# Two gathers for the left-over edges: accumulate in the DMA, or land in two halves and add on VectorE

## The chip, the cores and the metric

The kernel runs on one core of a Trainium2 chip. The metric is the device time of one execution in microseconds (us). Of the kernel before, three timed runs are given, 3217.1, 3209.39 and 3217.16 us, with a median of 3217.1 us. A fourth execution was profiled: it took 3212.38 us, with a span of 3210.7 us between its first and its last instruction and a mean granted TensorE clock of 0.993.

Five engines work side by side and meet at semaphores: TensorE (PE in the profile, PEld its weight loads), VectorE (DVE), ScalarE (ACT), GpSimd (POOL) and SyncE (SP). In this kernel SP issues the plain DMAs and POOL issues the indirect ones, the gathers.

## What is computed

The input is 64 graphs of 256 nodes with 256 features each, and one adjacency matrix for all of them, with few edges. Four layers run one after the other; layers 0, 1 and 3 are of one kind, layer 2 is an attention. Of the first kind, what matters here is the edge score S:

```python
pre_u = jnp.einsum('bud,dk->buk', h_t, W1[:d])
pre_v = jnp.einsum('bvd,dk->bvk', h_t, W1[d:])
hidden = jax.nn.relu(pre_u[:, :, None, :] + pre_v[:, None, :, :] + b1)
S = jax.nn.sigmoid(jnp.einsum('buvk,ko->buvo', hidden, W2)[..., 0] + b2[0])
a_t = jnp.einsum('buv,bud->bvd', S * A_a, h_t)
m_t = jnp.einsum('uv,bud->bvd', A_m, h_t) * h_t
z_t = beta1 * h_t + beta2 * (jnp.einsum('bvd,de->bve', a_t, Wa) + ba) + beta3 * (jnp.einsum('bvd,de->bve', m_t, Wm) + bm)
```

S is multiplied by A, so only the scores of edges that exist are needed. For each edge (u, v) that is a row of pre_u plus a row of pre_v, a relu, and a dot product with W2.

## The kernel before

Two graphs are worked on together, as a pair. Two streams of 16 pairs, "a" and "b", run interleaved. For each pair and each of the three layers with edge scores, `before` makes both projections and writes them to two tables in HBM (`tableu` and `tablev`, 256 rows each, one row for each node with both graphs side by side; SP, L750, one DMA for each table and each block of 128 rows). `scores` then makes the edge scores and `after` uses them. There are 16 x 2 x 3 = 96 such scorings. While one stream is in `scores`, which is heavy on VectorE, the other does its `after`, its attention and its next `before`, which are heavy on TensorE. The order of both on PE, DVE and ACT is written out by hand, one string for each kind of stage (`PLAN`): each letter runs one step of one generator, and `tc.manual_schedule` keeps that order on these three engines. R is the step `rest`, the one this study is about.

After the start the same six scorings come again every 195 us or so, 16 times. The texts below call them places 1 to 6, in order of time:

- place 1: the third layer of "b", under plan (LAST, "a"); place 2: the first layer of the next pair of "a", under (LAST, "b");
- place 3: the first layer of "b", under (GNN[0], "a"); place 4: the second layer of "a", under (GNN[0], "b");
- place 5: the second layer of "b", under (GNN[1], "a"); place 6: the third layer of "a", under (GNN[1], "b"). In places 5 and 6 the light stream does its attention.

The edges are cut into 16 blocks of 128. Ten blocks are made on TensorE, by one-hot matrices (`made`, into the PSUM tile `ga`). Six blocks (`FETCHED`) are gathered from the tables by indirect DMA into the SBUF tile `fetched`. Edges for which a block had no room, at most 64 for a graph, are the left-over edges: 128 rows for two graphs, of 256 elements, in the SBUF tile `left`. Each gathered block takes two gathers: one writes the rows of one table over the tile (`compute_op` bypass), the second adds the rows of the other table to it while it lands (`compute_op` add). `left` is made in the same way: `left<-tableu` writes, `left<-tablev` adds.

All gathers are issued by POOL in one order, that of `fetches_of`: `fetch` ties each one behind the one before it (`tc.issue_after`). Call the six blocks a to f. For each scoring the order is: u(a), u(b), v(c), v(d), then v(a) and v(b) that add, as soon as block 0 of the tables is written; then, once block 1 is written, `left<-tableu`, u(c) and u(d) that add, `left<-tablev` that adds, u(e), u(f), and v(e) and v(f) that add. An adding gather waits for the landing of the gather that wrote its tile. The two adding gathers of c and d stand between the two of `left`.

On VectorE the sum of each edge is worked off by one instruction for each 256 elements (`rated`: relu, times W2, and a running sum into a column of `raw`; the profile's group `junk<-...`). `rest` is one such instruction, on `left`. `rated_all` (steps E and Z) then makes the scores of `raw` on ScalarE (`val`), and `spread` brings them to the matrix `sa` by matmuls `ps<-rm,gu` and `ps<-ro,guo`.

The tile `left` has one buffer for each stream, as `puv` and the parts of it have. All those steps have line 104 in the profile (the helper that records the engine's last instruction), so groups are told apart by their tiles. The gathers have line 858.

Of the kernel before, what the change touches and what calls it, by code (L numbers as in the profile page):

```python
# [8 lines left out]
FP = mybir.dt.float32  # L9
# [3 lines left out]
ALU = mybir.AluOpType  # L13
AX = mybir.AxisListType

P = 128
B, N, D = 64, 256, 256
# [7 lines left out]
REST, DIAGONAL, BLOCKS = 0, 1, 5  # L25
# [21 lines left out]
def fetches_of(l):  # L47

    def part(b, x):
        y = 1 - x if places(b)[0] > places(b)[1] else x  # L50
        return b, x, y

    first, then = [], [(None, 0, 0)]
    for b in FETCHED[l]:
        one = [part(b, x) for x in range(2)]
        (first if min(places(b)) == 0 else then).append(one[0])
        (first if max(places(b)) == 0 else then).append(one[1])
    by = lambda p: p[1]
    first.sort(key=by)
    waiting = [p for p in then if p[0] and p[1] and min(places(p[0])) == 0]  # L60
    last = sorted((p for p in then if p[0] and p not in waiting), key=by)
    return [first, then[:1] + waiting + [(None, 1, 1)] + last]


PLAN = {
# [61 lines left out]
def adj_seq_kernel(ctx: ExitStack, tc: tile.TileContext, a: dict, out: bass.AP):  # L127
# [421 lines left out]
    def few(stack):  # L549
# [173 lines left out]
        def before(st, l):  # L723

            hT = st["hT"]
            st["puv"] = puv = one.tile([P, 2, 2, 2, D], FP, tag="puv", name="puv")
            st["parts"] = parts = [one.tile([P, 2, 2, 2 * D], FR, tag=f"part{k}" + st["side"], name=f"part{k}") for k in range(2)]
            order = [(m, g) for m in range(2) for g in range(2)]
            if l == LAST:
                order = [(m, g) for g in range(2) for m in range(2)]  # L730

            st["tables"] = [
                tables.tile([N, 2 * D], FP, tag="table" + t + st["side"], name="table" + t) for t in "uv"
            ]

            st["fetches"] = []
            st["fetched"] = {b: got_.tile([P, 2, D], FP, tag="fetched", name="fetched") for b in FETCHED[l]}
            st["left"] = one.tile([P, D], FP, tag="left" + st["side"], name="left")
            for m, g in order:
                if l == LAST and (m, g) == (1, 0):  # L740
                    st["flip"](1)
                t = psum()
                for c in range(2):
                    mm(out=t, lhsT=hT[:, c, g, blk(m)], rhs=w1[l][:, c], start=c == 0, stop=c == 1)
                scalar.copy(puv[:, m, 0, g, :], t[:, 0, :])
                vector.tensor_tensor(puv[:, m, 1, g, :], t[:, 1, :], b1row[l], ALU.add)
                if g == 1:
                    x = puv[:, m].rearrange("p w g d -> p (w g d)")
                    for w, rows in enumerate(st["tables"]):
                        nc.sync.dma_start(out=rows[blk(m)], in_=x[:, w * 2 * D : w * 2 * D + 2 * D])  # L750
                    st["fetches"] += fetches_of(l)[m]
                    if numbered:
                        fetch(st)
                    elif st not in unfetched:
                        unfetched.append(st)
                    yield
                    flat = [p[:, m].rearrange("p w d -> p (w d)") for p in parts]
                    for k, h in enumerate(halves):
                        scalar.copy(flat[k][h], x[h])
                    yield  # L760
                    for k, h in enumerate(halves):
                        vector.tensor_tensor(flat[k][halves[1 - k]], x[h], flat[k][h], ALU.subtract)
                yield

        def scores(st, l):

            raw = wk.tile([P, LATE.stop], FP, tag="raw", name="raw")
            val = wk.tile([P, LATE.stop], FP, tag="val", name="val")
            rm = one.tile([P, 2, 8, 2, 64], FP, tag="rm", name="rm")
            ro = one.tile([P, 2, N], FR, tag="ro", name="ro")  # L770
            st["val"], st["rm"], st["ro"] = val, rm, ro
            puv, parts = st["puv"], st["parts"]

            def rated(t, i):
                junk = wk.tile([P, D], FP, tag="junk", name="junk")
                vector.scalar_tensor_tensor(
                    junk, t, 0.0, w2row[l], ALU.max, ALU.mult, accum_out=raw[:, i : i + 1]
                )

            def both(t, *cols):  # L780
                for g in range(2):
                    rated(t[:, g, :], cols[g])

            def tile_scores(t, k, m, i):
                col = BLOCKS + 16 * m + 4 * k + i
                both(t, col, col + 8)

            def rated_all(cols, m):
                scalar.activation(val[:, cols], raw[:, cols], AF.Tanh, bias=halfb2[l], scale=0.5)
                scalar.add(val[:, cols], val[:, cols], 1.0)  # L790
                if m == 0:
                    wt = wk.tile([P, 3], FP, tag="wt", name="wt")
                    wh = wk.tile([P, 1], FR, tag="wh", name="wh")
                    vector.tensor_tensor(wt[:, 0:1], val[:, REST : REST + 1], awo, ALU.mult)
                    vector.tensor_copy(wh, wt[:, 0:1])
                    vector.tensor_tensor(wt[:, 1:2], wt[:, 0:1], wh, ALU.subtract)
                    for g, h in enumerate(halves):
                        for part, o in enumerate((h, halves[1 - g])):
                            scalar.mul(ro[o, g], gvo[h], wt[h, part : part + 1])
                of = slice(BLOCKS + 16 * m, BLOCKS + 16 * m + 16)  # L800
                vector.tensor_tensor(
                    rm[:, m], gva[:, m].rearrange("p k i v -> p (k i) v").unsqueeze(2).to_broadcast([P, 8, 2, 64]),
                    val[:, of].rearrange("p (g x) -> p x g", g=2).unsqueeze(3).to_broadcast([P, 8, 2, 64]), ALU.mult
                )

            def made():
                for k, m, i in sorted((b for b in ALL if b not in FETCHED[l]), key=lambda b: (b[1], b[2], b[0])):
                    n = PICKED.index((k, m, i))
                    t = ga.tile([P, 2, D], FP, tag="ga", name="ga")
                    mm(out=t, lhsT=pick_u[:, n, :], rhs=parts[k][:, m, 0], start=True, stop=False)  # L810
                    mm(out=t, lhsT=pick_v[:, n, :], rhs=parts[i % 2][:, i // 2, 1], start=False, stop=True)
                    tile_scores(t, k, m, i)
                    yield

            def got():
                for block in FETCHED[l]:
                    tile_scores(st["fetched"][block], *block)
                    yield

            def itself():  # L820
                for m in range(2):
                    x = puv[:, m].rearrange("p w g d -> p w (g d)")
                    own = one.tile([P, 2, D], FP, tag="own", name="own")
                    vector.tensor_tensor(own.rearrange("p g d -> p (g d)"), x[:, 0], x[:, 1], ALU.add)
                    both(own, DIAGONAL + 2 * m, DIAGONAL + 2 * m + 1)
                    yield

            def rest():
                rated(st["left"], REST)
                yield  # L830

            def early():
                rated_all(EARLY, 0)
                yield

            def late():
                rated_all(LATE, 1)
                yield

            return dict(  # L840
                T=made(), F=got(), O=itself(), R=rest(), E=early(), W=turned(st, l, ga), M=mixed(st, ga), Z=late()
            )

        def fetch(st):

            now, st["fetches"] = st["fetches"], []
            for block, x, y in now:
                rows, ids = st["tables"][y], (ids_u, ids_v)[y]
                if block is None:
                    to, ids = st["left"], (left_u, left_v)[x]  # L850
                    rows = rows.rearrange("n (g d) -> (n g) d", g=2)
                else:
                    f = SOME.index(block)
                    to, ids = st["fetched"][block].rearrange("p g d -> p (g d)"), ids[:, f : f + 1]
                    if places(block)[y] == 0:
                        rows = rows[blk(0)]
                with tc.issue_after(fetches[-1]) if fetches else nullcontext():
                    this = nc.gpsimd.indirect_dma_start(  # L858
                        out=to, out_offset=None, in_=rows, in_offset=bass.IndirectOffsetOnAxis(ap=ids, axis=0),
                        compute_op=(ALU.bypass, ALU.add)[x],  # L860
                    )
                fetches.append(this.ins)

# [191 lines left out]
```

## Time and profile before

| what | value |
|---|---|
| timed runs | 3217.1, 3209.39, 3217.16 us |
| the profiled execution | 3212.38 us, span 3210.7 us |
| gathers issued by POOL | 1344 (576 + 576 for blocks, 96 + 96 for left-over edges), 1868.5 us of POOL's 1875.2 us busy |
| DMA engines, mean busy share of the gathers' queue | 51.5% |
| VectorE, gathered blocks worked off (`junk<-fetched`) | 1152 instructions, mean 421 ns; idle before them 19.3 us in all |
| VectorE, blocks made on TensorE worked off (`junk<-ga`) | 1920 instructions, mean 419 ns; idle before them 3.1 us |
| VectorE, addition of 256 elements with one input in PSUM (`puv<-ps,L_gnn_b1row`) | 384 instructions, mean 421 ns |

The page lists, engine by engine, the busy time and then the chain of work that ended last: what would have to be shorter for the end to come sooner. A busy share is an average over places with different limits, so a change at one place is read from the chain and from the instructions in order of time at that place. Idle time of VectorE or POOL costs nothing as long as TensorE has work queued.

### The profile page before, as it was taken

To read this page: it belongs to the slowest core of one execution; us is meant where nothing else is said; L and a number is where in the kernel's file an instruction comes from. 1 tells how busy PE (TensorE), PEld (TensorE's weight loads), DVE (VectorE), ACT (ScalarE), POOL (GpSimd) and SP (SyncE) were. 2 spreads that over 40 slices of the span, in tenths; PEclk is the share of its full clock that TensorE was granted. 3 is DMA by queue.
4 is the path that set the end of the run, shared out by engine and by line. 5 is a ranking of instruction groups with operands and counts; after the bars stand their busy time and mean duration, and the time that the engine had idled before them with its cause. 6 is when DMAs were issued, how large, how long until landed. Compare 5 with 4: busy or idle time off the path is not lost.

```text
span 3210.7 us, 48619 instructions
## 1 busy us (share of the span) xinstructions
PE 3117.1 (97%) x14648; PEld 2230.7 (69%) x14648; DVE 2912.3 (91%) x10312; ACT 1359.1 (42%) x2658; POOL 1875.2 (58%) x1371
## 2 busy tenths in 40 slices
PE   6999999999999999999999999999999999999998
PEld 4667777677767667677677776767767676766766
DVE  6989999898999989999898998989989899898997
ACT  3444444434344443434444444344443434444342
POOL 2746566574756647556475564656656475664653
PEclk7999999999999999999999999999999999999999
DMA  5757676575756757667576675757667576675754
GB/s 151 150 127 184 133 178 141 143 173 126 190 132 164 166 117 185 140 159 164 128 183 134 164 155 134 177 128 177 139 150 170 121 188 134 163 166 115 184 134 96
DMA packets 231726, 486.59 MB, mean 152 GB/s; under 512 B 30880, under 2 KB 48160, under 8 KB 231456
## 3 DMA queue, kind: packets, MB, share of 16 engines
q0 software_dynamic: 147456, 327.24, 51.5%
q1 hardware_dynamic: 82416, 154.96, 13.6%
q8 instruction: 119, 1.95, 0.3%
q14 instruction: 151, 1.24, 0.1%
q10 hardware_dynamic: 1584, 1.20, 0.1%
HBM read 365.84 MB, written 117.44 MB: 151 GB/s over the span
## 4 chain that ended last, share of the span: by engine, by line
PE 58%; DVE 20%; issue 5%; DMA 5%; POOL 5%; ACT 4%; DVEq 0%; POOLq 0%
PE ps L104 38%; PE ga L104 20%; DVE junk L104 7%; DVE part L104 7%; POOL fetched L858 4%; DMA fetched<-tablev,ids_v 3%; DVE rm L104 2%; DMA fetched<-tableu,ids_u 1%; ACT logits L104 1%; POOL left L858 1%; DVE e L104 1%; ACT ro L104 1%; DMA left<-tablev,left_v 1%; DVE mT L104 1%; DVE puv L104 1%
## 5 line engine op out<-in xcount | busy, mean ns | idle before, releaser
L858 POOL DMA_INDIRECT fetched<-tableu,ids_u x576 | 737.3, 1280 | 880.1 <-DVE junk L104 298.3
L858 POOL DMA_INDIRECT fetched<-tablev,ids_v x576 | 873.8, 1517 | 335.7 <-DMA fetched<-tableu,ids_u 189.3
L104 PE MATMUL ps<-L_gnn_w,hT 128*128 128x512 f32 x1536 | 718.3, 599 | 9.1 <-DMA hT<-in_xT_dram 5.5
L104 DVE SCALAR_TENSOR_TENSOR junk<-ga,L_gnn_w2row 128x256 f32<-128x256 f32 x1920 | 714.6, 419 | 3.1
L104 PE MATMUL ga<-part,pick_u 128*128 128x512 f32 x960 | 518.2, 540 | 3.5 <-DVE junk L104 2.5
L104 DVE TENSOR_TENSOR part<-puv,part 64x1024 fp32r<-64x1024 f32 x384 | 468.7, 1221 | 12.7 <-ACT part L104 1.1
L104 ACT CAST part<-puv 64x1024 fp32r<-64x1024 f32 x384 | 401.0, 1044 | 166.7 <-DVE puv L104 161.8
L104 PEld LDWEIGHTS ps<-L_gnn_w,hT 128*128 128x128 f32 x1536 | 286.8, 191 | 263.3 <-issue 222.7
L104 DVE SCALAR_TENSOR_TENSOR junk<-fetched,L_gnn_w2row 128x256 f32<-128x256 f32 x1152 | 432.2, 421 | 19.3 <-DMA fetched<-tablev,ids_v 15.1
L104 PE MATMUL ga<-part,pick_v 128*128 128x512 f32 x960 | 379.5, 395 | 0.0
L104 PE MATMUL ga<-adj,h 128*128 128x256 f32 x1536 | 362.0, 380 | 3.7 <-issue 3.7
L104 PE MATMUL ga<-L_gnn_Wa,hT 128*128 128x256 f32 x1536 | 362.9, 379 | 0.0
L104 ACT COPY puv<-ps 128x256 f32<-128x256 f32 x384 | 139.7, 372 | 523.0 <-PE ps L104 392.6
L104 PEld LDWEIGHTS ga<-adj,h 128*128 128x128 f32 x1536 | 292.7, 191 | 79.5 <-issue 41.7
L104 PEld LDWEIGHTS ga<-L_gnn_Wa,hT 128*128 128x128 f32 x1536 | 289.9, 191 | 59.7 <-issue 22.0
L104 DVE TENSOR_TENSOR puv<-ps,L_gnn_b1row 128x256 f32<-128x256 f32 x384 | 156.6, 421 | 138.7 <-ACT puv L104 136.7
L104 PE MATMUL ps<-sa,hwa 128*128 128x256 f32 x1024 | 238.3, 380 | 0.0
L104 DVE TENSOR_TENSOR rm<-gva,val 128x1024 f32<-128x1024 f32 x192 | 234.8, 1223 | 3.5 <-ACT val L104 0.6
L104 PE MATMUL ps<-mT,L_gnn_Wm 128*128 128x512 f32 x512 | 235.5, 592 | 1.2 <-DVE mT L104 1.2
L104 PEld LDWEIGHTS ga<-part,pick_u 128*128 128x128 f32 x960 | 181.9, 190 | 75.7 <-issue 37.5
L104 ACT ACTIVATE ro<-gvo,wt 64x256 fp32r<-64x256 f32 x384 | 194.4, 506 | 89.1 <-DVE wt L104 84.3
L104 PEld LDWEIGHTS ga<-part,pick_v 128*128 128x128 f32 x960 | 182.0, 190 | 66.3 <-issue 41.1
(152 smaller groups left out, 4314.7 us busy)
## 6 DMA issues: line engine op xcount, KB each, us to landing
tableu<-puv SPq DMA_DIRECT2D x192, 256.0 KB, 3.0
tablev<-puv SPq DMA_DIRECT2D x192, 256.0 KB, 3.9
hT<-in_xT_dram SPq DMA_DIRECT2D x32, 512.0 KB, 5.9
h<-in_x_dram SPq DMA_DIRECT2D x64, 256.0 KB, 2.7
out_dram<-h SPq DMA_DIRECT2D x64, 256.0 KB, 4.2
fetched<-tableu,ids_u POOLq DMA_INDIRECT x576, 4.2
fetched<-tablev,ids_v POOLq DMA_INDIRECT x576, 5.2
L_gnn_w<-in_L_gnn_W_dram SPq DMA_DIRECT2D x6, 256.0 KB, 5.2
```

The costliest lines, as they stand in the source:

```text
L104: self.last = getattr(self.engine, op)(*a, **k)
L858: this = nc.gpsimd.indirect_dma_start(out=to, out_offset=None, in_=rows, in_offset=bass.IndirectOffsetOnAxis(ap=ids, axis=0), compute_op=( ...
```

## The change

The tile `left` becomes two halves of 256 elements. The gather of `tableu` lands in half 0, that of `tablev` in half 1, both with bypass. The second no longer stands behind the adding gathers of c and d but directly behind the first. `rest` first adds half 1 to half 0 on VectorE and then works off half 0 as before. In the built program the order of instructions on PE, ACT and SP is the same as before; VectorE has 96 instructions more, each just ahead of its `junk<-left`; on POOL `left<-tablev` comes two places earlier in each scoring. It no longer waits for `left<-tableu` to land. The new addition waits for both gathers, and `junk<-left` for the addition.

```diff
     waiting = [p for p in then if p[0] and p[1] and min(places(p[0])) == 0]
     last = sorted((p for p in then if p[0] and p not in waiting), key=by)
-    return [first, then[:1] + waiting + [(None, 1, 1)] + last]
+    return [first, then[:1] + [(None, 1, 1)] + waiting + last]
...
-            st["left"] = one.tile([P, D], FP, tag="left" + st["side"], name="left")
+            st["left"] = one.tile([P, 2, D], FP, tag="left" + st["side"], name="left")
...
             def rest():
-                rated(st["left"], REST)
+                left = st["left"]
+                vector.tensor_tensor(left[:, 0], left[:, 0], left[:, 1], ALU.add)
+                rated(left[:, 0], REST)
                 yield
...
-                    to, ids = st["left"], (left_u, left_v)[x]
+                    to, ids = st["left"][:, x], (left_u, left_v)[x]
...
-                        compute_op=(ALU.bypass, ALU.add)[x],
+                        compute_op=(ALU.bypass, ALU.add)[x if block else 0],
```

## The prediction

> **What bounds the kernel now.** I read the busy shares and the chain first, then the rows of the tile `left`, then at each of the six places the instructions and the chain in order of time.
>
> ```profile
> PE 3117.1 (97%) x14648; PEld 2230.7 (69%) x14648; DVE 2912.3 (91%) x10312; ACT 1359.1 (42%) x2658; POOL 1875.2 (58%) x1371
> PE 58%; DVE 20%; issue 5%; DMA 5%; POOL 5%; ACT 4%; DVEq 0%; POOLq 0%
> ```
>
> TensorE is full and most of the chain. But VectorE is nearly full as well and a fifth of the chain, and a tenth of it is POOL and DMA: the gathers. So the change touches three things that take turns at the end.
>
> ```profile
> L858 POOL DMA_INDIRECT left<-tableu,left_u x96: 984/994/1770, 70.0 to 3172.1; - x96
> L858 POOL DMA_INDIRECT left<-tablev,left_v x96: 1533/1535/1990, 75.0 to 3177.4; - x96
> L104 DVE SCALAR_TENSOR_TENSOR junk<-left,L_gnn_w2row x96: 409/422/492, 79.5 to 3187.4; 128x256 f32<-128x256 f32 x96
>   DMA left<-tablev,left_v: 13.5, 16
> ```
>
> Nanoseconds, least, median and most. The same 128 rows cost POOL 0.99 us as a plain gather and 1.54 as an adding one. The last row: VectorE waited 13.5 us for the second gather in the whole run, 16 times.
>
> Where the time is decided, by the chain. Place 4, in most rounds:
>
> ```profile
> 1296.73 1.53 POOL fetched L858
> ...
> 1298.57 1.75 POOL left L858
> 1300.32 0.30 issue
> 1300.62 3.74 DMA fetched<-tableu,ids_u
> ...
> 1305.09 4.82 DMA fetched<-tablev,ids_v
> ...
> 1320.86 1.24 DVE rm L104
> 1322.10 0.04 issue
> 1322.14 1.76 PE ps L104 x18
> ```
>
> (Start, length.) POOL's queue, with the adding gather of `left` in it, decides when block e lands; VectorE runs from there to `rm`, and TensorE stood idle 0.9 us before 1322.14. Places 5 and 6 are decided by VectorE and ScalarE; place 5:
>
> ```profile
> 1532.90 0.42 DVE logits L104
> ...
> 1533.68 0.75 DVE junk L104 x5
> ...
> 1536.09 0.08 DVE wt L104
> ...
> 1538.26 0.48 ACT logits L104
> ...
> 1538.78 8.11 PE ps L104 x28
> ```
>
> `junk<-left` starts at 1534.29, inside this stretch without a gap, and TensorE idles 0.52 us before 1538.78. Over the run TensorE waited so:
>
> ```profile
> PE ps L104 <- ACT logits L104: 27.2, 65, 0.7
> PE ps L104 <- DVE rm L104: 18.4, 27, 6.1
> ```
>
> At places 1 to 3 TensorE never idles (no gap from place 1 to place 4 in any round), and the chain stays on it. But VectorE runs there without gaps too, only just ahead:
>
> ```profile
> 1658.51 1.12 DVE L104 SCALAR_TENSOR_TENSOR sa<-diag,val,ps 128x128 f32<-128x128 f32 x4
> 1659.07 1.46 PE L104 MATMUL ps<-sa,hwa 128*128 128x256 f32 x6
> ```
>
> The first of the four takes 0.34 us and ends at 1658.85, the matmul that needs it starts at 1659.07: a lead of 0.22 us.
>
> **The change, part by part.** *The addition.* 96 of 256 elements, both inputs in SBUF, and `junk<-left` waits for each. The row like it is `own`, 512 elements, followed by its reader:
>
> ```profile
> 1516.88 0.69 DVE L104 TENSOR_TENSOR own<-puv 128x512 f32<-128x512 f32 x1
> 1517.61 0.43 DVE L104 SCALAR_TENSOR_TENSOR junk<-own,L_gnn_w2row 128x256 f32<-128x256 f32 x1
> ```
>
> 0.73 us from start to start. `part`, 1024 elements, takes 1.22, so an element costs (1.22 - 0.69) / 512 = 1.04 ns, and 256 fewer make 0.73 - 0.27 = 0.46 us. (The page's `puv` row, 256 elements, has 0.421; with the 0.035 before a dependent reader that is 0.456.) 96 x 0.46 = 44 us of VectorE's time. What of it is paid:
>
> - Places 5 and 6, 32 additions. The path is VectorE without gap, then ScalarE, then a TensorE that is idle and waiting (at 6: `junk<-left` at 1569.51, the row `e` behind it, TensorE's waits of 0.17 and 0.22 us at 1570.25 and 1571.67). Paid in full: 32 x 0.46 = 14.7 us.
> - Places 1 to 3, 48 additions, 1.38 us a round. VectorE's own idle there, in the round from 1419 us, is 0.14, 0.29 and 0.16 us before instructions that wait for TensorE's or ScalarE's results; late, it skips some of these. The leads over TensorE go down to 0.15 (`rm`) and 0.22, plus 0.1 or so for the matmul then in the array. So of 1.38 about 0.6 goes into its idle and 0.1 to 0.25 into a lead that stays used up, and TensorE has to wait the rest: I take 0.7 a round, 11.2 us. Ends: 0 if the leads hide all, 22 if none.
> - Place 4: VectorE waits there for gathers anyway. In the four rounds of 16 in which it hardly does, 0.3 each: 1 us.
>
> *The gather as bypass, placed earlier.* POOL needs 0.99 for 1.54: 0.55 us a scoring, 53 us of POOL in all, behind which u(e), u(f), v(e), v(f) stand. Only place 4 is bound by that. TensorE's idle there, 18 to 19 us after `junk<-left`, adds up to 6.0 us in 12 rounds (0.12 to 0.94), the most there is to gain. 0.55 a round would bring 5.0; part is eaten, as places 1 to 3 bring VectorE late to the table's second block, which starts this row of gathers: I take 3. Lower end: the added instruction has two SBUF inputs, as `part`, `rm` and `own`; plain gathers that overlapped one of these took 1.20 us on average, the others 1.01. If the addition delayed POOL by its whole 0.42, 0.13 of 0.55 would be left and the gain near 0.
>
> *The wait for `left` goes.* The second gather is issued 1.3 us after the first instead of 5.0 to 5.9 and lands some 4 us earlier; VectorE comes 9.2 us after the first gather's issue at the earliest, and a gather of `left` takes 3.4 to 5.5 to land. So all 13.5 us of waiting vanish. Of these 5.0 us (five rounds) lie at place 6, on the path: gained in full. 7.4 lie at place 4, where the next wait, for e, takes their place; counted above. The rest, 1.3, is in the first scoring; with POOL's shorter list in the first three I take 1.5.
>
> *Moved later:* the adding gathers of c and d, by 0.99 + 0.30 = 1.3 us. VectorE takes c and d no sooner than 8.5 us after their issue, and a landing is 4.8 in the chain above: 7.2 is left, nothing paid. *The queue passed:* the second gather needs the store of `tablev`'s second block sooner; if that is late, c to f wait behind it on POOL. It would be issued 5.5 us or more after the store's issue, and a store lands in 3.9 (median): covered, with 1.6 to spare.
>
> [...]
>
> **Sum.** 14.7 + 11.2 + 1 - 3 - 5.0 - 1.5 = +17.4 us on the profiled execution's 3212.4: 3229.8. That execution is 4.7 us below the median of the runs and within their spread (3209.4 to 3217.2); the mean of all four is 3214.0, which makes 3231.4. I say 3231.
>
> **Rivals.**
>
> - *Hidden:* at places 1 to 3 all is absorbed, and the gains are at their ends: 14.7 - 6.0 - 5.0 - 2.4 = +1.3, 3215. For it: no TensorE gap at places 1 to 3 today. Against: leads of 0.15 to 0.5 us under a lag of up to 1.38.
> - *Faster:* POOL's list is what decides, and the additions of places 5 and 6 fit before a ScalarE or TensorE that is late anyway: -6.0 - 5.0 - 2.4 = -13.4, 3199 to 3201. It decides once another input of `e` and of the first `ACT ro` arrives 0.46 us or more after VectorE's. For it: a tenth of the chain is POOL and DMA. Against: in both chains the step before is VectorE itself.
> - *VectorE alone:* places 1 to 3 pay all, with lags that run on into place 4: 44 - 5.0 - 1.5 = +37, 3250. It decides if the leads are used up by late rounds. Against: VectorE's 15 us idle in a round.
> - *Not what it says:* the second gather still waits for the first to land. POOL would stand 2.6 us (3.9 less 1.3) in 96 scorings, and place 4 would pay it: 16 x 2.6 = +42 on top, 3270. The built program names no such wait.
>
> **How the numbers follow.** Less than 0.3% (10 us) can't be told from no change. Forecast (+8 to +28) 0.60, of which 0.05 falls within 0.3%; hidden 0.22; faster 0.10; VectorE alone 0.05; not as said 0.03. So slower 0.55 + 0.08 = 0.63, same 0.05 + 0.22 = 0.27, faster 0.10. The likeliest's own range is 3222 to 3244; the range to hold 8 of 10 takes in most of "hidden" below and the upper end of places 1 to 3 (22 for 11.2) above: 3213 to 3246.
>
> **What would show it.** `left<-tablev` at 0.99 us median and no wait of VectorE for it. An addition of 0.42 us, `junk<-left` 0.46 after it. Rounds longer by about 1 us, with TensorE's new idle at places 1 to 3 behind `rm`, `sa` or `mT`, and the waits at place 6 gone. I am wrong if TensorE shows no gap at places 1 to 3, or if the rounds' stretch over places 5 and 6 is not 0.9 us longer.

## The result

The changed kernel takes 3256.24 us (median of 4, 3254.16 to 3261.8), the kernel before 3215.09 (four runs). The ratio is 1.0128, 95% interval 1.0114 to 1.0143: slower by 41 us, well over the 0.3% that can be told from no change. The forecast of slower was right, the size was not: 3231 was forecast, with 3213 to 3246 as its range. The profiled execution took 3257.54 us, with a span of 3255.8.

The busy times and the chain of the changed kernel:

```profile
PE 3133.1 (96%) x14648; PEld 2226.1 (68%) x14648; DVE 2950.4 (91%) x10408; ACT 1360.1 (42%) x2658; POOL 1826.7 (56%) x1371
PE 69%; DVE 19%; issue 4%; ACT 4%; DMA 3%; POOL 1%; DVEq 0%; SPq 0%; POOLq 0%
```

POOL has lost 48.5 us of work and fallen from 5% of the chain to 1%, DMA from 5% to 3%; VectorE has 38 us more. So the work moved as foreseen, and the chain runs over TensorE more than before. The rows of the tile `left` (least, median and most in ns):

```profile
L860 POOL DMA_INDIRECT left<-tableu,left_u x96: 989/991/1660, 70.4 to 3216.8; - x96
L860 POOL DMA_INDIRECT left<-tablev,left_v x96: 966/971/1257, 71.7 to 3218.1; - x96
L104 DVE TENSOR_TENSOR left<-left x96: 410/418/427, 79.9 to 3232.1; 128x256 f32<-128x256 f32 x96
L104 DVE SCALAR_TENSOR_TENSOR junk<-left,L_gnn_w2row x96: 424/425/458, 80.4 to 3232.6; 128x256 f32<-128x256 f32 x96
```

The second gather costs 0.97 us instead of 1.54, the addition 0.42; VectorE no longer waits for `left` at all. What is new stands among the waits (us in total, times, longest). First VectorE's for ScalarE's copy `sa`, before and in the changed kernel:

```profile
DVE sa L104 <- ACT sa L104: 4.4, 10, 1.6
...
DVE sa L104 <- ACT sa L104: 24.2, 27, 1.8
```

Then TensorE's of the changed kernel:

```profile
PE ps L104 <- ACT logits L104: 34.6, 65, 1.0
PE ps L104 <- DVE sa L104: 19.5, 20, 1.6
PE ps L104 <- DVE rm L104: 10.1, 12, 6.3
```

The wait for `logits` has grown by 7.4 us (27.2 before): that is place 5's addition, 16 x 0.46. TensorE's wait for `sa` was 1.0 us in 2 times before. Both waits for `sa` belong to `spread`, where the scores of the left-over edges enter by the matmuls `ps<-ro,guo`; the PSUM result is then copied into `sa` by ScalarE and read by VectorE. "The spread of place 3" below is the one of that place's scores; it runs as the scoring of place 4 begins, and the gathers issued beside it are those for place 4. One of them in the kernel before (start, length, engine):

```profile
1490.24 1.54 POOL L858 DMA_INDIRECT fetched<-tableu,ids_u  x1 [0.30 <-issue]
...
1491.43 0.73 PE L104 MATMUL ps<-ro,guo 128*128 128x512 f32 x2
...
1491.97 0.65 ACT L104 COPY sa<-ps 128x256 f32<-128x256 f32 x2 [3.82 <-PE ps L104]
```

The adding gather of c, the first row, is over at 1491.78. The first of the two matmuls ends at 1491.93, and the copy starts 0.04 us after that. The same spread in the changed kernel:

```profile
1515.97 0.73 PE L104 MATMUL ps<-ro,guo 128*128 128x512 f32 x2
1516.11 1.69 POOL L860 DMA_INDIRECT fetched<-tableu,ids_u  x1 [0.30 <-issue]
...
1516.54 0.40 PE L104 MATMUL ga<-part,pick_u 128*128 128x512 f32 x1
...
1517.24 0.40 PE L104 MATMUL ga<-part,pick_v 128*128 128x512 f32 x1
1517.66 0.65 ACT L104 COPY sa<-ps 128x256 f32<-128x256 f32 x2 [4.90 <-PE ga L104]
1518.07 0.86 DVE L104 SCALAR_TENSOR_TENSOR sa<-diag,val,ps 128x128 f32<-128x128 f32 x3 [1.00 <-ACT sa L104]
...
1518.47 0.48 PE L104 MATMUL ps<-sa,hwa 128*128 128x256 f32 x1 [0.84 <-DVE sa L104]
```

The first `ps<-ro,guo` ends at 1516.46 by the profile, ScalarE was idle and needs nothing else, and yet its copy starts at 1517.66, 1.20 us late. The second row is the adding gather of block c: POOL issues it from 1516.11 to 1517.80. TensorE goes on meanwhile with four matmuls `ga`, then it has to wait for `sa`. Of the six matmuls from the first `ps<-ro,guo` on, five send a semaphore update. These are recorded at 1517.64, 1517.67, 1517.71, 1517.74 and 1517.79, within 0.15 us, though the matmuls end at 1516.46 to 1517.63. Matmuls that follow one another by 0.23 us cannot all end within 0.15 us, so it is the updates that are late. Below, a "late copy" is a first `sa<-ps` of a spread that starts over 0.3 us after that matmul's end, and what delays it is called the hold-up. The kernel before has none in its profile (all start 0.04 us after it); the changed one has 26 in 96, 15 of them at place 3, and over all 96 the delays beyond 0.04 us add up to 37.6 us.

Where the time went, by stretches from one spread to the next, each summed over the last 15 rounds (14 for the one that crosses the end of a round). The last column anticipates the run `t1_changed`: the same kernel on another chip.

| stretch up to the spread of | forecast | result, less before | changed kernel on chip 7, less before |
|---|---|---|---|
| places 1, 2, 3 | +11.2 | +3.5, +8.5, +4.1 | +0.6, +8.9, +0.4 |
| place 4 | -2 | **+14.5** | -2.1 |
| place 5 | +7.4 | +6.9 | +6.9 |
| place 6 | +2.3 | +2.5 | +1.5 |
| start, to the seventh spread | -1.5 | +5.3 | +2.4 |
| sum | +17.4 | +45.3 | +18.6 |

The stretch that begins with the spread of place 3 is the miss: +14.5 for -2. Both columns are taken against the one profile of before, with its span of 3210.7 us. So they show where the two changed profiles differ, by 26.7 us in all and 16.6 at place 4. They do not show what the change costs on chip 7: there the kernel before takes 3202 us (median), and the change costs 27.

### The profile page after: what moved, and what is told of

It reads as the page before. It is cut to its first block, busy times and chain, and to the rows that moved or that the text cites. A ratio compares the mean times of both kernels' runs of the same rounds, so it can differ in the third digit from the quotient of the medians.

```text
span 3255.8 us, 48544 instructions
## 1 busy us (share of the span) xinstructions
PE 3133.1 (96%) x14648; PEld 2226.1 (68%) x14648; DVE 2950.4 (91%) x10408; ACT 1360.1 (42%) x2658; POOL 1826.7 (56%) x1371
## 3 DMA queue, kind: packets, MB, share of 16 engines
q14 instruction: 150, 1.23, 0.1%
## 4 chain that ended last, share of the span: by engine, by line
PE 69%; DVE 19%; issue 4%; ACT 4%; DMA 3%; POOL 1%; DVEq 0%; SPq 0%; POOLq 0%
PE ps L104 46%; PE ga L104 24%; DVE junk L104 8%; DVE part L104 4%; DMA fetched<-tablev,ids_v 2%; ACT ro L104 1%; DVE e L104 1%; ACT logits L104 1%; DVE rm L104 1%; POOL fetched L860 1%; DVE h L104 1%; DVE own L104 1%; DVE mT L104 1%; DVE puv L104 1%; DVE logits L104 1%
## 5 line engine op out<-in xcount | busy, mean ns | idle before, releaser
L104 DVE SCALAR_TENSOR_TENSOR junk<-fetched,L_gnn_w2row 128x256 f32<-128x256 f32 x1152 | 431.6, 420 | 14.5 <-DMA fetched<-tablev,ids_v 9.2
L104 PEld LDWEIGHTS ga<-part,pick_u 128*128 128x128 f32 x960 | 181.9, 189 | 76.7 <-issue 37.6
L104 PEld LDWEIGHTS ps<-sa,hwa 128*128 128x128 f32 x1024 | 190.1, 190 | 63.4 <-DVE sa L104 34.6
```

What stands on the lines that cost most here:

```text
L104: self.last = getattr(self.engine, op)(*a, **k)
```

## The experiments

18 runs on five chips. Each ratio is to the kernel before on the same chip, with its 95% interval; the last column counts late copies.

| run | edit | chip | ratio | late |
|---|---|---|---|---|
| e1_wider | before, `left` twice as wide | 9 | 1.0001 (0.9992 to 1.0009) | 9 |
| e2_addonly | before, one more VectorE instruction | 9 | 1.0082 (1.0069 to 1.0095) | 5 |
| e3_order | before, adding gather of `left` moved up | 9 | 1.0431 (1.0414 to 1.0449) | 1 |
| e4_oldorder | changed, gathers in the old order | 9 | 1.0070 (1.0058 to 1.0082) | 6 |
| e5_noadd | changed, no addition | 5 | 0.9990 (0.9981 to 0.9999) | 0 |
| e7_plainfirst | changed, e and f ahead of c and d | 5 | 1.0072 (1.0058 to 1.0086) | 0 |
| e8_before_plainfirst | before, e and f ahead | 5 | 1.0288 (1.0274 to 1.0302) | 0 |
| e9_between | changed, second gather between c and d | 5 | 1.0069 (1.0055 to 1.0082) | 0 |
| r1_changed_again | changed | 15 | 1.0147 (1.0129 to 1.0165) | 25 |
| r2_before_again | before | 15 | one execution, 3201.98 us | 7 |
| e10_pooladd | changed, addition on POOL | 15 | 1.0190 (1.0176 to 1.0204) | 30 |
| s1_changed | changed | 12 | 1.0077 (1.0063 to 1.0090) | 0 |
| s2_noadd | as e5_noadd | 12 | 0.9982 (0.9973 to 0.9991) | 0 |
| s3_plainfirst | as e7_plainfirst | 12 | 1.0064 (1.0050 to 1.0078) | 0 |
| s4_between | as e9_between | 12 | 1.0066 (1.0052 to 1.0079) | 0 |
| t1_changed | changed | 7 | 1.0081 (1.0068 to 1.0094) | 0 |
| t2_noadd | as e5_noadd | 7 | 0.9996 (0.9987 to 1.0005) | 0 |
| t3_plainfirst | as e7_plainfirst | 7 | 1.0074 (1.0061 to 1.0087) | 0 |

### Which part of the change

**Addresses.** Only the width of `left`:

```diff
-            st["left"] = one.tile([P, D], FP, tag="left" + st["side"], name="left")
+            st["left"] = one.tile([P, 2, D], FP, tag="left" + st["side"], name="left")
...
-                rated(st["left"], REST)
+                rated(st["left"][:, 0], REST)
```

> The kernel before, with the tile `left` twice as large and only its first half used: nothing but SBUF addresses moves. Three theories of the 41 us that the change costs. Addresses (the tiles behind `left` lie elsewhere, and the matmul `ps<-ro,guo` ends late for that): 3230 to 3235 us, with ScalarE's copy `sa<-ps` late behind `ps<-ro,guo` by more than 0.3 us in some 30 of 96 cases. Additions (VectorE's 96 x 0.46 us alone): 3215, no late copy. Order (the adding gathers of c and d now run beside the spread of the scores): 3215, no late copy.

1.0001. Addresses cost nothing; that theory has fallen. But nine late copies appear, in a kernel with the same instructions as the one before, whose profile had none. Seven are at place 3, most of them 0.47 to 0.62 us long.

**The addition alone.**

```diff
             def rest():
-                rated(st["left"], REST)
+                left = st["left"]
+                vector.tensor_tensor(left, left, left, ALU.max)
+                rated(left, REST)
```

> The kernel before, with one more VectorE instruction of 256 elements ahead of each `junk<-left` (left = max(left, left), which leaves it as it is); gathers, order and addresses as before. Additions: 3250 to 3260, late copies as in the changed kernel. Order: 3240 to 3250 (the additions at places 1 to 3, 5 and 6 without the gains), no late copy. Addresses: 3235 to 3245, no late copy.

1.0082, which is 28 us by the medians (3232.75 and 3204.45). The instruction has the size of the real one:

```profile
L104 DVE TENSOR_TENSOR left<-left x96: 408/419/431, 79.9 to 3208.4; 128x256 f32<-128x256 f32 x96
```

So 28 of VectorE's 44 us are paid. The ranges were reckoned from 3215, and this chip has 3204: against that, +28 is what "order" expected (25 to 35) and "addresses" too, and less than "additions" did (35 to 45). The late copies stay at five: the additions alone do not make them.

**The order alone**, the second gather still adding, so that it waits:

```diff
-    return [first, then[:1] + waiting + [(None, 1, 1)] + last]
+    return [first, then[:1] + [(None, 1, 1)] + waiting + last]
```

> The kernel before, with the adding gather of `left` moved directly behind the writing one, no addition on VectorE. It has to wait for the landing, some 2.6 us, and all gathers behind it with it. Order: 16 x 2.6 = +42 at place 4 and late copies besides, above 3257. Additions and addresses: +42 at most, less what is hidden in front of e, 3230 to 3257, no late copy.

1.0431, 140 us: far above what any theory said. The wait by itself was sized rightly (2.8 us each), in the waits of POOL:

```profile
POOL left L858 <- DMA left<-tableu,left_u: 268.8, 95, 4.6
```

What I had wrong is who pays: +53 us in the stretch up to place 4 and +61 in the one up to place 2, 3.6 and 4.4 a round. A gather list later by 2.8 us is more than the cover at place 2 as well. Part of what exceeds 2.8 us a round is the clock: the granted clock of this profile is 0.985, for 0.994 of `e1_wider` on the same chip. It has 16 stretches of 3.4 us at half the clock, each beside a gap of TensorE of 1.2 to 3.3 us; the profile of before has none but in its first 100 and its last 20 us. At half speed they cost at most 16 x 3.4 / 2 = 27 us, an estimate.

With one late copy the run says nothing of the hold-up, but it shows that the new place needs the bypass.

**Halves and addition, old order.**

```diff
-    return [first, then[:1] + [(None, 1, 1)] + waiting + last]
+    return [first, then[:1] + waiting + [(None, 1, 1)] + last]
```

> The changed kernel with the gathers in the order of before: both of `left` write into halves, VectorE adds, the adding gathers of c and d stand between the two again. Order: 3235 to 3242, few late copies, and the stretch from the spread of place 3 to that of place 4 back near that of before. Additions or addresses: 3250 to 3262, late copies as in the changed kernel.

1.0070, six late copies: the changed kernel without its order costs 23 us here, where the result's chip paid 41 with it. It seemed to settle that the order makes the late copies.

**No addition; two other orders.** In e5 the addition's line is left out. The other two change the list, first e7, then e9; e8 puts e and f ahead in the kernel before:

```diff
-    return [first, then[:1] + [(None, 1, 1)] + waiting + last]
+    return [first, then[:1] + [(None, 1, 1)] + last[:2] + waiting + last[2:]]
...
+    return [first, then[:1] + waiting[:1] + [(None, 1, 1)] + waiting[1:] + last]
```

> The changed kernel without the addition on VectorE: `junk<-left` works off half 0 alone, so the rows of `tablev` are left out of the left-over edges' scores. POOL's order is that of the change, VectorE's that of before. Collision (an adding gather whose issue begins about when the matmul `ps<-ro,guo` ends holds up ScalarE's `sa<-ps` until that issue is over; the change moves the gather of c there): ratio to before about 1.004 to 1.006, 41 us less the 26 of the additions, with 20 or more late copies, most of them at place 3. Lateness (the collisions come from VectorE's additions): about 0.998, only the gains of places 4 and 6, late copies as seldom as in the kernel before on the same chip (9 of 96).

> The changed kernel with another order on POOL: both gathers of `left`, then the plain gathers of e and f, then the adding ones of c and d, then those of e and f. At place 3 a plain gather now stands where the adding one of c stood. Collision: late copies gone at place 3 (fewer than 8 in all), ratio about 1.004 to 1.007, the additions' 26 us less what place 4 gains by the earlier landing of e, up to 6. If plain gathers hold up the copy as well, or the later place of c and d costs: 1.012 and above.

> The changed kernel with the second gather of `left` between the adding ones of c and d. The adding gather of c is then issued when it was before. Collision: ratio about 1.007 as with the gathers in the old order, late copies below 10 (at place 3 the matmul ends inside the gather of c or in front of the plain one of `left`). If the place of the second gather costs by itself: 1.010 or more.

> The kernel before with the plain gathers of e and f directly behind the writing gather of `left`, then the adding ones of c, d and `left`, then those of e and f. No addition on VectorE, no halves. If the landing of e is what bounds place 4: faster by up to 6 us, ratio 0.998, with fewer late copies than before on the same chip. `left` is whole 2.6 us later, so VectorE's wait for it at places 6 and 4 grows from 13.5 us: up to 16 x 2.6 = +42 us at place 6, ratio up to 1.013. I take 1.003.

The order without the addition costs nothing (0.9990), and no late copy appears in any of the four. That looked like the "lateness" reading of e5, and it fits e7 and e9. But in e5 at place 3 the gather of c was issued, in nine rounds of 16, from 0.42 us before the matmul's end to 1.26 after it, much as in nine rounds of the changed kernel (0.35 before to 1.34 after), and held up nothing. So something else than the kernel differed. The miss of e8 has nothing to do with it: `left` is whole 2.6 us later, and VectorE's wait for it grows from 13.5 to

```profile
DVE junk L104 <- DMA left<-tablev,left_v: 87.5, 41, 4.3
```

with +47 us up to place 6 and +27 up to place 4, against the profile of before. Here too the clock adds to it: 0.986, with eleven stretches at half the clock, 44 us in all, up to place 6. The adding gather of `left` may not come later than it does.

### The chip

> The changed kernel once more, unaltered, beside the kernel before, since all variants with the addition came out at 1.007 to 1.008 and none of the last four had a late copy. Collision as a property of the order together with the addition: ratio about 1.013 again, some 30 late copies, 15 of them at place 3. Collision as something that comes and goes with the chip or the occasion: ratio 1.006 to 1.008, late copies fewer than 8, as with the other variants.

> The kernel before once more, for a profile on the same chip as the run next to it: within 0.3% of the other runs of this kernel here. Collision as something of the occasion: late copies of the same sort (none, or a few) as in the changed kernel next to it.

On chip 15 the changed kernel costs 1.0147, with 25 late copies, 16 at place 3; the kernel before has seven on the same chip. Then all beside one another on chip 12:

> The changed kernel for the third time, now on the same chip as the next three. Hold-ups of the kernel: 1.013 to 1.015 with some 25 late copies, whatever the chip. Hold-ups of the occasion: either that, and late copies in the next three as well, or about 1.007 with none here and none there.

> The new order without the addition (the rows of `tablev` left out of the left-over scores) once more, beside the changed kernel. Hold-ups of the occasion, and this is one that has them: about 1.004 with 15 or more late copies at place 3, as its adding gather of c covers the same moment (issue from 0.42 us before the matmul's end to 1.26 after it). Otherwise 0.999 and none.

> The changed kernel with the plain gathers of e and f ahead of the adding ones of c and d once more, beside the changed kernel. If adding gathers alone hold up: 1.007 and fewer than 8 late copies whether the others have them or not. If plain gathers do so too on such an occasion: 1.010 or more, late copies at place 3.

> The changed kernel with the second gather of `left` between the adding ones of c and d once more, beside the changed kernel. Its gather of c covers the moment as that of the kernel before does: 1.007, and at most some 8 late copies of about 0.5 us.

The changed kernel has no late copy here and costs 1.0077. The intervals of the three kernels with the addition overlap: between these three orders no difference can be told on this chip. Once more, on chip 7:

> The changed kernel for the fourth time, as the measure of the next two. On a chip with hold-ups: 1.013 to 1.015, some 25 late copies. On one without: 1.007 to 1.008 and none.

> The new order without the addition (the rows of `tablev` left out of the left-over scores). On a chip with hold-ups: the order alone costs 1.003 to 1.006, with late copies at place 3, as its gather of c covers the same moment without the addition too; if it takes the addition, 0.998 to 0.999 with fewer than 10. On a chip without: 0.998 to 0.999 and none.

> The changed kernel with the plain gathers of e and f ahead of the adding ones of c and d. On a chip with hold-ups: 1.007 to 1.008 and fewer than 8 late copies if only adding gathers hold up; 1.010 or more, late copies at place 3, if plain ones do too. On a chip without: 1.006 to 1.007 and none.

1.0081, 0.9996, 1.0074 and none late. The timeline of `t1_changed` on chip 7, at the same spread as the one shown above (the window begins inside the matmuls, so it shows the second):

```profile
1502.89 1.69 POOL L860 DMA_INDIRECT fetched<-tableu,ids_u  x1 [0.31 <-issue]
...
1503.07 0.40 PE L104 MATMUL ps<-ro,guo 128*128 128x512 f32 x1
1503.27 0.65 ACT L104 COPY sa<-ps 128x256 f32<-128x256 f32 x2 [3.74 <-PE ps L104]
...
1503.76 1.12 DVE L104 SCALAR_TENSOR_TENSOR sa<-diag,val,ps 128x128 f32<-128x128 f32 x4
...
1504.24 2.77 PE L104 MATMUL ps<-sa,hwa 128*128 128x256 f32 x12
```

The gather of c starts 0.34 us before the first matmul's end at 1503.23 and takes 1.69 us, as above. But the copy starts 0.04 us after that end, and `ps<-sa,hwa` 1.01 after it, where the chip of the result needed 2.01: one microsecond lost in that round's place 3. The five updates of TensorE are recorded at 1503.25, 1503.48, 1503.72, 1503.95 and 1504.42, each as its matmul ends. The waits of TensorE on chip 7:

```profile
PE ps L104 <- ACT logits L104: 34.6, 65, 1.0
PE ps L104 <- DVE rm L104: 20.5, 40, 6.3
...
PE ps L104 <- DVE sa L104: 1.0, 2, 0.6
```

The wait for `sa` is gone; what stays is that for `logits` (places 5 and 6) and one for `rm`.

So the hold-up goes with the chip or with the occasion: on 9 and 15, and in the result, it is there in every profile; on 5, 7 and 12 in none of eleven. The profile of before had none. Each chip was used on one occasion only, so the two cannot be told apart; "chip" below means either. Beside the kernel before on the same chip, the change costs 44 us on chip 15, 23 on 12 and 27 on 7.

What the kernel adds to it is the moment. On chips 9 and 15 the kernel before (`e1_wider`, `r2_before_again`) has its late copies at place 3 where the gather of c begins 0.7 to 1.1 us before the matmul's end, so that its issue is over 0.4 to 0.9 after it. In the changed kernel it stands behind one more plain gather (0.97 us and 0.30 between) and begins from 0.36 before to 0.27 after the end, but for two rounds, and is over only 1.3 to 1.8 us after.

The late copies follow this moment round by round. In the four runs that have the old order on chips 9 and 15 (`e1_wider`, `e2_addonly`, `e4_oldorder`, `r2_before_again`), the gather of c lies across the end of the matmul at place 3 in 7, 5, 6 and 7 rounds of 16. In each of these 25 the copy is 0.46 to 0.94 us late, in none of the other 39 by more than 0.2. On the chips without hold-ups the gather lies across it as well (6 rounds in `e9_between`, 4 in `s4_between`), and no copy is late. In 43 of the 51 late copies of the result and of `r1_changed_again` the issue of an adding gather ends within 0.25 us of the copy's start.

The old order avoids most of it: `e4_oldorder`, on a chip with hold-ups, has 1.0070 and six late copies, where the changed kernel has 1.0147 and 25 on chip 15. The changed kernel itself was not run on chip 9.

Not shown: whether the order alone, without the addition, costs anything on such a chip, or whether the orders of `e7_plainfirst` and `e9_between` avoid it there; all of those runs were on chips without hold-ups. Nor is every hand-over beside an adding gather held up. In the result 32 copies `hwa<-ga` by ScalarE and 27 instructions `e<-ps` by VectorE stood waiting for a matmul that ended within such an issue, most of them that of e or f, and none started over 0.17 us after it. What sets `ps<-ro,guo` apart is open.

### The addition on POOL

```diff
+                if block and (block, x) == then_add[0]:
+                    left = st["left"]
+                    with tc.issue_after(fetches[-1]):
+                        this = nc.gpsimd.tensor_tensor(left[:, 0], left[:, 0], left[:, 1], ALU.add)
+                    fetches.append(this.ins)
```

(`then_add[0]` is the plain gather of f.)

> The changed kernel with the addition on POOL, behind the plain gather of f and ahead of the adding one of e, where POOL waits for the landing of e's first rows anyway; VectorE has no instruction more than before. If VectorE's time is what the change costs: the 26 us go and some 3 us of gain stay, ratio 0.998 to 1.000. If POOL's addition takes over 2.6 us, or waits for `left`, place 4 pays and `junk<-left` at place 6 comes later: 1.003 to 1.010.

1.0190, on chip 15, so 16 us worse than the changed kernel there (3268.41 and 3252.27). The place on POOL is hidden as foreseen, and VectorE waits for the sum only twice. It pays otherwise. The rows of the tile `own` in this run, whose instructions have both inputs in SBUF:

```profile
L104 DVE SCALAR_TENSOR_TENSOR junk<-own,L_gnn_w2row x384: 412/424/1525, 40.9 to 3232.7; 128x256 f32<-128x256 f32 x192
...
L104 DVE TENSOR_TENSOR own<-puv x192: 675/686/1246, 40.2 to 3231.6; 128x512 f32<-128x512 f32 x192
```

The longest are 1.5 and 1.2 us. Beside POOL's addition (0.75 us), `junk<-own` took 1.08 us on average (24 times), `junk<-fetched` 1.02 (41) and `own` 1.23 (20), for 0.42, 0.42 and 0.69 otherwise; `junk<-ga`, which reads PSUM, stayed at 0.42 (85). That makes 24 x 0.66 + 41 x 0.60 + 20 x 0.54 = 51 us of VectorE, more than the 40 us of additions taken away. These 11 us do not make the 16; the rest is not taken apart. The longest lengthening, 1.1 us, exceeds the 0.75 of the POOL instruction beside it; why, no run here shows.

No version here beats the kernel before: the only ones at or below 1.000 leave out the rows of `tablev`.

## Why the prediction was wrong in size

**Places 5 and 6: right.** Paid in full, 0.46 us each: without the addition and with it (chips 7 and 12) the two stretches differ by 6.7 to 6.9 and by 7.1 us in 15 rounds. In ten rounds of the result both stretches together are 0.9 to 1.1 us longer, as the prediction asked for; in the other five the end of the wait for `left` takes that back in part or in whole, as it also said.

**Places 1 to 3: right in sum, not in place.** The same pairs give 9.5 us on chip 7 and 11.5 on chip 12; I took 11.2. But nearly all of it is at place 2 (9.1, 0.65 a round), at most 1.9 at place 1 and 0.6 at place 3. I had spread it evenly. TensorE's new gaps at place 2 (over 0.1 us) are behind `rm`, in 14 rounds on chip 7, where the profile of before has none.

**The wait for `left` and place 4: right in the profile, smaller on other chips.** The new order without the addition gains 5.6 us up to place 6 and 4.2 up to place 4 against the profile of before. But the 13.5 us of waiting for `left` differ from profile to profile: 7.8 us in `e1_wider` on chip 9 and 6.3 in `r2_before_again` on chip 15. So beside the kernel before on the same chip the gain is 1 to 5 us (0.9996, 0.9990, 0.9982), and with the 28 of the addition the change costs 1.0077 to 1.0081 there.

**The start: wrong.** Not 1.5 us gained but 2.4 lost on chip 7, 5.3 in the result; I had counted the gain of POOL and not the additions of the first scorings on their way to the seventh spread (3.4 us on chip 7, with and without them). "The queue passed" was not covered every time either: POOL waited for the store of `tablev` ahead of its gathers of `left` for 5.8 us in six times, 0.3 in one before. What that cost is not taken apart.

**The step that failed** is this one: "Moved later: the adding gathers of c and d, by 0.99 + 0.30 = 1.3 us ... nothing paid." I asked who takes their rows and when, and found 7.2 us left for a landing of 4.8. I did not ask beside what the issue itself comes to stand. It came to stand on the end of `ps<-ro,guo` at place 3, and where the hand-over from that matmul to ScalarE is held up until such an issue ends, that costs about 1 us in each round: +14.5 for -2 in that stretch, and the few us more at places 1 and 3. By the sum of the table, all else came to +18.6 for +17.4. That nearness is in part luck: terms missed in both directions, and beside the kernel before on its own chip 7 the change costs 27 us. The profile of before could not have shown the price, since no copy was late in it; a profile of the same kernel from another chip could. Why such a chip holds this hand-over up is open.

**The rivals.** "Hidden" fails at place 2, where 0.65 us a round is paid, and "faster" altogether: no run with all its rows is faster. "VectorE alone", 3250, is nearest to the result, but not by its mechanism: the addition alone took 28 us, not 44. "Not what it says" is measured by e3_order: on chip 9 the order with a second gather that waits costs 140 us, not the 42 that I gave the wait, since place 2 pays too (+61 us) and the granted clock is 0.985 for 0.994.

## What to carry to other kernels

An issue on POOL that is moved has to be costed three times: for its reader, for the queue behind it, and for what runs beside it at its new moment, above all where an engine hands over a result that another is waiting for: here ScalarE's copy came up to 2.05 us late. An addition on an engine that is 91% busy and just ahead of the bound costs what each place shows, here 28 of 44 us; and moving it to POOL cost VectorE 51 us for the 40 saved in `e10_pooladd`, in instructions whose inputs are both in SBUF (`junk<-ga`, which reads PSUM, stayed at 0.42 us). A difference of a per cent between two profiles should be looked for on a second chip before the kernel is blamed.

## What was not expected of the hardware

- On chips 9 and 15 and in the result ScalarE's copy behind `ps<-ro,guo` starts late, and TensorE's semaphore updates come in a burst, at the end of an adding gather's issue on POOL: five in 0.15 us, up to 2.05 us after the matmul's end in the result. TensorE itself goes on, with four matmuls `ga` in the round shown. In the result 176 of TensorE's recorded updates come over 0.06 us after the end of the last matmul that sends one, of VectorE's 2 and of ScalarE's 2; in the profile of before it is 2 of each. In the result the copies `hwa<-ga` and `puv<-ps` that stood waiting for TensorE start at most 0.17 us after it; what holds up `sa<-ps` is open.
- In the traces with hold-ups 3569 to 3751 updates of TensorE are recorded (3588 in `r2_before_again`), in the others 4138 to 4145 (4143 in the profile of before), for the same count of matmuls: the chips can be told apart by this alone. It is not TensorE's matter alone: of VectorE's updates 5525 are recorded in the result and 6393 in `t1_changed`, of ScalarE's 2039 and 2376. A missing record need not be a delay: in the result eight readers (five `hwa<-ga`, one each of `e<-ps`, `mT<-ga` and `junk<-ga`) stood waiting for a matmul that has no record within 0.06 us of its end, and seven of them started 0.04 us after that end, one 0.17. Whether the recording takes part in the hold-up, no run here can tell.
- In `e10_pooladd` POOL's addition of 256 elements lengthened VectorE's instructions beside it by up to 1.1 us, more than its own 0.75.
